# Node order worked out in eight pieces inside the loop over h, with ScalarE taking half of each node's row

## The chip, the cores and the metric

The kernel runs on one core of a Trainium2 chip. A core has five engines that run side by side and wait for one another through semaphores: TensorE (PE, with its weight loads shown apart as PEld), VectorE (DVE), ScalarE (ACT), GpSimd (POOL) and SyncE (SP). The last three can also issue DMAs. The metric is the device time of one execution in microseconds; lower is better.

## The reference, cut to what matters

Four layers of a graph network over 2048 nodes and 8 batches of 64 features. Only the start of the first layer matters here:

```python
h = x @ W                                     # (8, 2048, 64)
s = leaky_relu(h @ a_node, 0.2)
alpha = softmax(where(H.T > 0, s, NEG))       # weights of the nodes in each of 64 hyperedges
agg = einsum('ben,bnf->bef', alpha, h)        # what the edges gather from their nodes
beta = sigmoid((h @ a_gn)[:, None, :] + (agg @ a_ge)[:, :, None])
all_he = elu(beta * h + (1 - beta) * agg)     # one row for each pair of node and edge
```

A later stage (here the mixing stage) needs, for each node, a row with h scaled by `exp(h @ a_gn)`, and it needs the nodes sorted by how many edges they belong to, so that tiles of 128 nodes have equal numbers of edges.

## The kernel before, in words

**The loop over h (lines 597 to 645)** goes over 16 tiles of 128 nodes, `t` = 0 to 15. In each round:

- PE multiplies the tile of x by the weights: four matmuls into the PSUM tile `ph` (line 600). `ph` has two buffers; each fills two PSUM banks, k = 0 and k = 1, with four batches each.
- DVE clips the two score columns into `seen` (line 611); ACT takes the exponential of one of them into `e_gn`, which is part of the row tile `st` (line 616); DVE makes the leaky relu `lr` (618) and ACT its exponential into `ex` (622).
- DVE writes the node's row into `st`, (h + 1) · e_gn, with one instruction of 256 columns for each bank (625), and h times the softmax weight into `ex` (629).
- PE adds `ex` into the edges' sums `pagg` with two matmuls (637).
- POOL copies the slot numbers into `st` (614). `st` holds two tiles and has three buffers, so a buffer is free again when the store from three pairs ago has landed.
- In odd rounds ACT's queue issues the store of two tiles of rows, `hs_hbm` (635). After rounds 1, 3, 5, 7 and 9 POOL copies one element of `seen` (`behind`, line 482) and then issues a 512 KB load of the adjacency, `load_adj` (211): that copy is what paces the loads. After rounds 9 and 11 `parts` splits a block of x in two (ACT cast, line 167, and POOL subtraction, line 168).

**The nodes' order.** After round 9, `place()` (lines 553 to 590) works out the sorted position of each node: ten small DVE instructions, one large DVE comparison (`ohq`, 128x2048, line 578), 16 small matmuls into `po` (582) and two more DVE instructions, which write `order`.

**After the loop**, POOL gathers the sorted rows from `hs_hbm` with indirect DMAs (`fetch_rows`, line 275), which need `order` and all eight stores, and issues the remaining loads of the adjacency (tiles 10 to 15, columns half 0, then half 1 a few at a time). DVE, ACT and PE turn `pagg` into the edges' tables (lines 672 to 733): `den`, `agg`, `he`, `tab`, then scores `pse`, then `ts`. The first mixing step needs `ts` (line 717) and one-hot matrices `o` (line 294), which are made from the slot numbers of the first gathered row tile (`pslot`, `slot`, lines 285 to 288).

From there on PE interleaves the mixing steps with the products of the adjacency (`ug`, lines 383 to 418), a fixed number of them behind each step, and the later layers follow.

**What sets the order of the work.** Each engine runs its instructions in the order in which they stand on its queue. A scheduler decides that order when the program is built, except for instructions that are wrapped in `tc.keep_in_program_order`, which stay in the order of the program on their engine. In the loop of the kernel before, only ACT's exponential of `lr` is wrapped (line 621); `mm` (line 171) is a matmul that is wrapped.

Of the kernel before, what the change touches and what calls it, by code (L numbers as in the profile page):

```python
# [30 lines left out]
F32 = mybir.dt.float32  # L31
F32R = mybir.dt.float32r
BF16 = mybir.dt.bfloat16
# [3 lines left out]
AF = mybir.ActivationFunctionType  # L37
ALU = mybir.AluOpType
AX = mybir.AxisListType
# [17 lines left out]
def tile_gnn_fast(  # L57
# [24 lines left out]
    nc = tc.nc  # L82
    B, N, F = out.shape
    E = h_nt.shape[2]
    D = emb.shape[1]
    P = 128
    NT = N // P
# [116 lines left out]
    order = hy.tile([P, NT], U32, name="order")  # L204
# [130 lines left out]
    def fetch(p, c, eng=nc.sync):  # L335
        xc[p, c] = staged("xc")
        load_x(xc[p, c], p, c, eng)

    def parts(p, c):
        part[c] = split(va, xc.pop((p, c)), f"v{c}", 1, [P, JT, P], nc.gpsimd, p == 0)  # L340
# [94 lines left out]
    with tc.tile_pool(name="pa_ps", bufs=1, space=PSUM) as pps:  # L435
# [10 lines left out]
        m_n = pa.tile([P, NT, E], F32, name="m_n")  # L446
# [18 lines left out]
        so = so_scope.enter_context(tc.tile_pool(name="so", bufs=1))  # L465
# [4 lines left out]
        iota = so.tile([P, P], BF16, name="iota")  # L470
        nc.gpsimd.iota(iota, [[1, P]], base=0, channel_multiplier=0, allow_small_or_imprecise_dtypes=True)
        row = so.tile([P, 1], F32, name="row")
# [8 lines left out]
        def behind(what):  # L481
            tc.keep_in_program_order(nc.gpsimd.tensor_copy(seen_x, what))
# [6 lines left out]

        for c in range(2):  # L490
            fetch(0, c, nc.gpsimd)
        paced = {1: 5, 3: 6, 5: 7, 7: 8, 9: 9}

        pw = pps.tile([P, 2], F32, tag="sm", name="pw", bufs=2)
        nc.tensor.matmul(pw, lhsT=w0t, rhs=a2, start=True, stop=True)
        for b in range(2):
# [21 lines left out]
            flat, lhsT=tri, rhs=oh.rearrange("p t b -> p (t b)"), start=True, stop=False  # L518
        )
        for t in range(NT - 1):  # L520
            nc.tensor.matmul(
                flat[:, (t + 1) * BINS:], lhsT=ones_b,
                rhs=oh[:, t:t + 1, :].to_broadcast([P, NT - 1 - t, BINS]), start=False, stop=False,
            )
        nc.tensor.matmul(
            flat, lhsT=ones_b, rhs=gtb[:, None, :].to_broadcast(bins), start=False, stop=True
# [4 lines left out]
        rank = so.tile([P, NT], F32, name="rank")  # L531
        nc.vector.tensor_reduce(rank, gt, AX.X, ALU.add)

        over = so.tile([P, BINS], F32, name="over")
# [9 lines left out]
        for t in range(NT // 2):  # L544
            for k in range(2):
                r = slice(k * E, (k + 1) * E)
# [3 lines left out]
        slot = pa.tile([P, NT, E], BF16, name="slot")  # L550
        nc.vector.tensor_tensor(slot, pcm, m_n, ALU.mult)

        def place():

            tl = so.tile([P, NT], F32, name="tl")
            ge = so.tile([P, NT, NT], F32, name="ge")
            tc.keep_in_program_order(
                nc.vector.tensor_scalar(over[:, 0:NT], iota[:, 0:NT], float(P), -0.5, op0=ALU.mult, op1=ALU.add)
            )
            wide = [P, NT, NT]  # L560
            nc.vector.tensor_tensor(
                ge, rank[:, :, None].to_broadcast(wide), over[:, None, 0:NT].to_broadcast(wide), ALU.is_gt
            )
            nc.vector.tensor_reduce(tl, ge, AX.X, ALU.add)
            nc.vector.tensor_scalar(tl, tl, -1.0, None, op0=ALU.add)
            q = so.tile([P, NT], F32, name="q")
            nc.vector.scalar_tensor_tensor(q, tl, -float(P), rank, op0=ALU.mult, op1=ALU.add)
            nc.vector.tensor_tensor(
                ge, tl[:, :, None].to_broadcast(wide), iota[:, None, 0:NT].to_broadcast(wide), ALU.is_equal
            )  # L570
            val = so.tile([P, NT, 2, NT], BF16, name="val")
            nc.vector.tensor_tensor(
                val[:, :, 0, :], ge, iota[:, 0:NT, None].to_broadcast(wide), ALU.mult
            )
            nc.vector.tensor_scalar(val[:, :, 1, :], ge, row, None, op0=ALU.mult)
            po = pps.tile([P, 2, NT], F32, tag="sm", name="po", bufs=2)
            ohq = so.tile([P, NT, P], BF16, name="ohq")
            nc.vector.tensor_tensor(
                ohq, q[:, :, None].to_broadcast([P, NT, P]), iota[:, None, :].to_broadcast([P, NT, P]), ALU.is_equal
            )  # L580
            for t in range(NT):
                nc.tensor.matmul(
                    po.rearrange("p i t -> p (i t)"), lhsT=ohq[:, t, :],
                    rhs=val[:, t].rearrange("p i t -> p (i t)"), start=t == 0, stop=t == NT - 1,
                )
            olo = so.tile([P, NT], F32, name="olo")
            nc.vector.tensor_copy(olo, po[:, 1, :])

            nc.vector.scalar_tensor_tensor(order, olo, float(NT), po[:, 0, :], op0=ALU.mult, op1=ALU.add)
            so_scope.close()  # L590


        seen = pa.tile([P, NT, B, 2], F32, name="seen")

        pagg = pps.tile([P, C], F32, tag="agg", name="pagg", bufs=1)
        G = B // 2
        for t in range(NT):
            ph = pph.tile([P, 2, C], F32, tag="ph", name="ph", bufs=2)
            for p in range(NP):
                nc.tensor.matmul(  # L600
                    ph[:, p // 2, (p % 2) * 2 * (F + 2):(p % 2 + 1) * 2 * (F + 2)], lhsT=xt[t][:, p, :],
                    rhs=bd66.rearrange("p b f -> p (b f)"), start=True, stop=True,
                )
            fetch_xt(t + 2 * XB)
            hv = ph[:, :, 0:G * (F + 2)].rearrange("p k (g c) -> p k g c", c=F + 2)
            if t % 2 == 0:
                st2 = pa.tile([P, 2, HROW], F32, tag="st", name="st", bufs=3)
            st = st2[:, t % 2]
            ex = pa.tile([P, 2, G, F + 1], F32, tag="ex", name="ex", bufs=2)
            sv = seen[:, t].rearrange("p (k g) c -> p k g c", k=2)  # L610
            nc.vector.tensor_scalar(
                sv, hv[:, :, :, F:F + 2], CLIP, -CLIP, op0=ALU.min, op1=ALU.max
            )
            nc.gpsimd.tensor_copy(st[:, BF + 8:], slot[:, t, :])
            e_gn = st[:, BF:BF + 8]
            nc.scalar.activation(e_gn.rearrange("p (k g) -> p k g", k=2), sv[:, :, :, 1], AF.Exp)
            lr = pa.tile([P, B], F32, tag="lr", name="lr", bufs=2)
            nc.vector.scalar_tensor_tensor(
                lr, seen[:, t, :, 0], 0.2, seen[:, t, :, 0], op0=ALU.mult, op1=ALU.max
            )  # L620
            tc.keep_in_program_order(
                nc.scalar.activation(ex[:, :, :, F], lr.rearrange("p (k g) -> p k g", k=2), AF.Exp)
            )
            for k in range(2):
                nc.vector.scalar_tensor_tensor(
                    st[:, k * G * F:(k + 1) * G * F].rearrange("p (g f) -> p g f", f=F), hv[:, k, :, 0:F], 1.0,
                    e_gn[:, k * G:(k + 1) * G, None].to_broadcast([P, G, F]), op0=ALU.add, op1=ALU.mult,
                )
            nc.vector.tensor_tensor(
                ex[:, :, :, 0:F], hv[:, :, :, 0:F], ex[:, :, :, F:F + 1].to_broadcast([P, 2, G, F]), ALU.mult  # L630
            )
            if t == 9:
                place()
            if t % 2:
                nc.scalar.dma_start(hs_hbm.rearrange("(p t) c -> p t c", t=NT)[:, t - 1:t + 1, :], st2)
            for k in range(2):
                nc.tensor.matmul(
                    pagg[k * E:(k + 1) * E, 0:G * (F + 1)], lhsT=m_n[:, t, :], rhs=ex[:, k].rearrange("p g c -> p (g c)"),
                    start=t == 0, stop=t == NT - 1,
                )  # L640
            if t in paced:
                behind(seen[:, t, 0, 0:1])
                load_adj(paced[t], 0)
            if t in (9, 11):
                parts(0, (t - 9) // 2)
        nc.vector.tensor_reduce(
            wrong[:, 2:3], seen.rearrange("p t b c -> p (t b c)"), AX.X, ALU.max, apply_absolute_value=True
        )
# [93 lines left out]
    with ExitStack() as pb_scope:  # L742
        pps = pb_scope.enter_context(tc.tile_pool(name="pb_ps", bufs=1, space=PSUM))
# [311 lines left out]
    for i in range(steps + 1):  # L1055
        k = 9 if i > NCH else 8
# [536 lines left out]
    for u in range(2, UNITS):  # L1593
        c, k = divmod(u, 2)
# [134 lines left out]
    place = ["g"] * NCH  # L1729
# [63 lines left out]
    for p in range(NP):  # L1793
# [3 lines left out]
        for step in range(STEPS):  # L1797
            last = step == STEPS - 1
            w_v, bias = (bd_v, b1) if step == 0 else (bd_v2, b1s)
            if p == 0 and step == 0:  # L1800
                opened = opening()
            for g in range(2):
# [16 lines left out]
                for mine in ([[c] for c in own] if very_end else [own]):  # L1819
                    for t in range(NT if p or step else 0):  # L1820
                        if checks and t in (2, 7, 12):
                            check()
                        for i in range(2):
                            for c in mine:
                                mm(
                                    u[c], lhsT=x_part[t // JT][i][:, t % JT, :], rhs=adj_c(t, c),
                                    start=False, stop=t == NT - 1 and i == 1,
# [765 lines left out]
```

## Time and profile before

| what | us |
|---|---|
| median of 3 runs | 1750.76 (1748.91 to 1751.80) |
| the profiled execution's own time | 1754.68 |
| its span | 1752.8 |
| PE busy in the span | 1670.7 (95%) |
| DVE, ACT, POOL busy | 855.4, 600.9, 572.4 |
| first `seen` of the loop over h starts | 14.45 |
| last store of rows is issued | 55.63 |
| last `pagg` starts | 56.12 |
| first gather of sorted rows is issued | 59.28 |
| first one-hot matrix of the mixing stage starts | 65.27 |

Times of single events are counted from the start of the span. A row of the timeline gives start, duration (of the whole group where it ends in xN), engine, line, operation, output and inputs, shapes, and in brackets how long the engine had been idle and what ended that. In the table of stretches, each line gives the busy time of PE, PEld, DVE, ACT and POOL with the number of instructions, the clock that was granted to TensorE (1.00 is full), the share of the DMA engines' time and the rate of the DMAs.

### The profile page before, as it was taken

Reading aid. Unit: us, or ns where it says so; the run is one execution under the profiler, and the core shown is the slowest. Engines: PE = TensorE matmul, PEld = TensorE weight load, DVE = VectorE, ACT = ScalarE, POOL = GpSimd, SP = SyncE. Lnnn points to the kernel's source line nnn. Section 1 sums busy time; section 2 is a strip of 40 time slices with the busy share of each in tenths; the row PEclk is TensorE's granted clock in tenths of the full one; section 3 lists DMA queues with packets and bytes.
Section 4 is the critical chain, followed back from the end, with each engine's and each line's share of the span. In section 5 each row is a group of like instructions: output and inputs, shape, how many; then the busy total and the mean of one; then the engine's idle time right before and its main releaser. Section 6 shows DMA issues by size and latency. Waiting matters only on the chain. (4 is left out here: it accounts for less than half of the span.)

```text
span 1752.8 us, 28206 instructions
## 1 busy us (share of the span) xinstructions
PE 1670.7 (95%) x11196; PEld 1214.0 (69%) x11196; DVE 855.4 (49%) x1583; ACT 600.9 (34%) x1123; POOL 572.4 (33%) x515
## 2 busy tenths in 40 slices
PE   6888899999889999999999999999989999999996
PEld 4666666666664444468788877777767877878775
DVE  7679945678742221210137158888723433433332
ACT  1345524434221211111213158888612222222221
POOL 4578845556534443422023001222310200202001
PEclk9899999999989999999999989999999999999998
DMA  9743344444340000027344467576481121211211
GB/s 328 252 161 124 101 130 140 152 143 144 99 135 6 30 19 12 24 69 292 109 137 130 115 134 153 125 162 139 126 295 42 49 60 44 61 43 44 59 42 39
DMA packets 171182, 195.84 MB, mean 112 GB/s; under 512 B 71536, under 2 KB 116336, under 8 KB 169760
## 3 DMA queue, kind: packets, MB, share of 16 engines
q1 hardware_dynamic: 160096, 154.54, 30.3%
q0 software_dynamic: 8544, 30.68, 5.2%
q10 hardware_dynamic: 2400, 8.72, 1.4%
q8 instruction: 90, 1.47, 0.3%
q14 instruction: 52, 0.43, 0.1%
HBM read 126.72 MB, written 67.17 MB: 111 GB/s over the span
## 5 line engine op out<-in xcount | busy, mean ns | idle before, releaser
L172 PE MATMUL ua<-pt,xn 128*128 128x512 f32 x512 | 230.2, 592 | 1.4 <-DVE pt L1150 1.4
L1488 ACT COPY w_half<-pw 128x512 f32<-128x512 f32 x316 | 191.3, 687 | 44.9 <-PE pw L172 43.4
L172 PEld LDWEIGHTS ua<-pt,xn 128*128 128x128 f32 x512 | 96.9, 190 | 111.1 <-issue 104.0
L1490 DVE COPY w_half<-pw 128x512 f32<-128x512 f32 x196 | 133.7, 715 | 72.7 <-PE pw L172 70.2
L172 PE MATMUL py<-w_half,xg 128*32 128x128 f32 x4096 | 142.6, 281 | 0.0
L172 PE MATMUL u<-adj,v0h 128*128 128x512 f32 x384 | 134.0, 426 | 1.1 <-ACT h L1788 1.1
L172 PE MATMUL u<-adj_more,v2h 128*128 128x512 f32 x384 | 126.5, 408 | 0.0
L172 PE MATMUL u<-adj_more,v2l 128*128 128x512 f32 x384 | 125.0, 403 | 0.0
L172 PE MATMUL u<-adj,v0l 128*128 128x512 f32 x384 | 124.5, 402 | 0.0
L172 PEld LDWEIGHTS py<-w_half,xg 128*32 128x32 f32 x4096 | 111.8, 138 | 17.4 <-issue 0.4
L172 PE MATMUL pw<-est,wst 64*128 64x256 f32 x1024 | 118.3, 324 | 4.1 <-DMA est<-est_hbm 2.3
L1156 POOL TENSOR_TENSOR acc<-acc,pt 128x512 f32<-128x512 f32 x60 | 76.5, 1276 | 104.2 <-DVE pt L1150 103.5
L172 PEld LDWEIGHTS pw<-est,wst 64*128 64x128 f32 x1024 | 82.8, 189 | 35.6 <-issue 18.5
L1150 DVE TENSOR_SCALAR pt<-pt 128x512 f32<-128x512 f32 x64 | 29.7, 465 | 152.6 <-ACT pt L1149 152.4
L1697 ACT CAST ar<-fcav 128x512 fp32r<-128x512 f32 x64 | 39.5, 618 | 166.7 <-DMA fcav<-in_adj_t 162.0
L1698 DVE SCALAR_TENSOR_TENSOR ar<-fcav,ar 128x512 f32<-128x512 f32 x64 | 45.6, 713 | 101.2 <-ACT ar L1697 101.0
L172 PE MATMUL u<-adj,v1h 128*128 128x512 f32 x288 | 94.6, 407 | 0.0
L1149 ACT ACTIVATE pt<-s 128x512 f32<-128x512 f32 x64 | 38.0, 598 | 164.5 <-PE s L172 164.5
L172 PE MATMUL u<-adj_more,v3l 128*128 128x512 f32 x288 | 93.9, 401 | 0.0
L172 PE MATMUL u<-adj_more,v3h 128*128 128x512 f32 x288 | 93.2, 402 | 0.0
L172 PE MATMUL u<-adj,v1l 128*128 128x512 f32 x288 | 92.7, 400 | 0.0
L1669 POOL TENSOR_TENSOR x<-x,rows 128x512 f32<-128x512 f32 x16 | 22.5, 1432 | 210.6 <-PE pt L175 200.2
(405 smaller groups left out, 3220.0 us busy)
## 6 DMA issues: line engine op xcount, KB each, us to landing
fcav<-in_adj_t SPq DMA_DIRECT2D x64, 256.0 KB, 2.9
u_hbm<-ut SPq DMA_DIRECT2D x48, 256.0 KB, 2.6
xg<-u_hbm SPq DMA_DIRECT2D x24, 512.0 KB, 9.0
adj<-in_adj_t POOLq DMA_DIRECT2D x16, 512.0 KB, 7.6
adj_more<-in_adj_t POOLq DMA_DIRECT2D x16, 512.0 KB, 7.5
adj_hbm<-adj_more SPq DMA_DIRECT2D x16, 512.0 KB, 6.1
x_hbm<-r SPq DMA_DIRECT2D x28, 256.0 KB, 2.8
hs_hbm<-st ACTq DMA_DIRECT2D x8, 584.0 KB
```

The source lines that it names most:

```text
L172: tc.keep_in_program_order(nc.tensor.matmul(*args, **kw))
L1149: nc.scalar.activation(pt, s, AF.Exp)
L1150: nc.vector.tensor_scalar(pt, pt, 1.0, None, op0=ALU.max)
L1156: nc.gpsimd.tensor_tensor(accs[c], accs[c], pt, ALU.add)
L1488: pin(nc.scalar.copy(dst, src))
L1490: pin(nc.vector.tensor_copy(dst, src))
L1669: nc.gpsimd.tensor_tensor(xs, xs, b2.to_broadcast([P, JT, P]), ALU.add)
L1697: nc.scalar.copy(ar, seen_a)
L1698: nc.vector.scalar_tensor_tensor(ar.bitcast(F32), seen_a, 1.0, ar.bitcast(F32), op0=ALU.mult, op1=ALU.not_equal, accum_out=left[:, t, k:k ...
```

## The change

Four things are done in the loop over h.

- `place()` is cut into eight pieces that are put at the ends of rounds 4 to 11: `find_tile` (4), `tile_columns` (5), four pieces of `row_columns` with a quarter of `ohq` each (6 to 9), `turn_order` with the 16 matmuls (10), `write_order` (11).
- The half of a node's row in bank k = 1 is written by ACT, with one instruction of 64 columns for each of four batches: `Identity(scale · h + bias)` with scale and bias both the column `e_gn` of that batch. DVE keeps the half in bank k = 0.
- The loop's instructions on PE, DVE and ACT are wrapped so that they stay in the program's order, and the program issues `pagg` of round t - 1 in round t (`gather`).
- Four more loads of the adjacency are paced in the loop, tiles 10 to 13, behind `seen` of rounds 11, 12, 13 and 14.

In the order of the built program, PE's instructions stand as before, except that the 16 `po` matmuls come one round earlier. DVE goes round by round: `seen`, `lr`, `st`, `ex`, then the round's piece. ACT goes `e_gn`, `ex`, four Identities, and in odd rounds the store's issue. The first of the four Identities waits for DVE's half of the same row. On POOL the copies of slots for rounds 6 and 7 now stand ahead of the pacing copy of round 3, and the four loads stand ahead of the first gather.

```diff
-        paced = {1: 5, 3: 6, 5: 7, 7: 8, 9: 9}
+        paced = {1: 5, 3: 6, 5: 7, 7: 8, 9: 9, 11: 10, 12: 11, 13: 12, 14: 13}
...
-        def place():
...
+        hold = tc.keep_in_program_order
+        def find_tile():
+            hold(nc.vector.tensor_scalar(over[:, 0:NT], iota[:, 0:NT], float(P), -0.5, op0=ALU.mult, op1=ALU.add))
+            hold(nc.vector.tensor_tensor(ge, rank..., over..., ALU.is_gt))
+            hold(nc.vector.tensor_reduce(tl, ge, AX.X, ALU.add))
+            hold(nc.vector.tensor_scalar(tl, tl, -1.0, None, op0=ALU.add))
+            hold(nc.vector.scalar_tensor_tensor(q, tl, -float(P), rank, op0=ALU.mult, op1=ALU.add))
+        def tile_columns():       # ge, then two halves of val
...
+        def row_columns(i):
+            r, quarter = slice(i * NT // 4, (i + 1) * NT // 4), [P, NT // 4, P]
+            hold(nc.vector.tensor_tensor(ohq[:, r, :], q[:, r, None]..., iota..., ALU.is_equal))
+        def turn_order():         # 16 matmuls into po
...
+        def write_order():        # olo, order
...
+        placing = {4: find_tile, 5: tile_columns, 10: turn_order, 11: write_order}
+        for i in range(4):
+            placing[6 + i] = lambda i=i: row_columns(i)
...
-            for k in range(2):
-                nc.vector.scalar_tensor_tensor(st[...], hv[:, k, :, 0:F], 1.0, e_gn[...], op0=ALU.add, op1=ALU.mult)
-            nc.vector.tensor_tensor(ex[:, :, :, 0:F], hv[:, :, :, 0:F], ex[:, :, :, F:F + 1]..., ALU.mult)
-            if t == 9:
-                place()
+            hold(nc.vector.scalar_tensor_tensor(st[:, 0:G * F]..., hv[:, 0, :, 0:F], 1.0, e_gn[:, 0:G, None]..., op0=ALU.add, op1=ALU.mult))
+            for g in range(G, B):
+                one = e_gn[:, g:g + 1]
+                hold(nc.scalar.activation(st[:, g * F:(g + 1) * F], hv[:, 1, g - G, 0:F], AF.Identity, bias=one, scale=one))
+            hold(nc.vector.tensor_tensor(ex[:, :, :, 0:F], hv[:, :, :, 0:F], ex[:, :, :, F:F + 1]..., ALU.mult))
+            if t in placing:
+                placing.pop(t)()
+            if t > 0:
+                gather(t - 1)
```

More of the change, by code (lines that the diff above doesn't have):

```diff
@@ L551, in tile_gnn_fast @@
         nc.vector.tensor_tensor(slot, pcm, m_n, ALU.mult)
-        def place():
[L555 to L580, printed above, removed]
@@ new lines, in tile_gnn_fast @@
+        wide_t = [P, NT, NT]
+        tl, q, olo = (so.tile([P, NT], F32, name=name) for name in ("tl", "q", "olo"))
+        ge = so.tile(wide_t, F32, name="ge")
+        val = so.tile([P, NT, 2, NT], BF16, name="val")
+        ohq = so.tile([P, NT, P], BF16, name="ohq")
+        po = pps.tile([P, 2, NT], F32, tag="sm", name="po", bufs=2)
+        hold = tc.keep_in_program_order
+        def find_tile():
+            hold(nc.vector.tensor_scalar(over[:, 0:NT], iota[:, 0:NT], float(P), -0.5, op0=ALU.mult, op1=ALU.add))
+            hold(nc.vector.tensor_tensor(
+                ge, rank[:, :, None].to_broadcast(wide_t), over[:, None, 0:NT].to_broadcast(wide_t), ALU.is_gt
+            ))
+            hold(nc.vector.tensor_reduce(tl, ge, AX.X, ALU.add))
+            hold(nc.vector.tensor_scalar(tl, tl, -1.0, None, op0=ALU.add))
+            hold(nc.vector.scalar_tensor_tensor(q, tl, -float(P), rank, op0=ALU.mult, op1=ALU.add))
@@ new lines, in tile_columns @@
+        def tile_columns():
+            hold(nc.vector.tensor_tensor(
+                ge, tl[:, :, None].to_broadcast(wide_t), iota[:, None, 0:NT].to_broadcast(wide_t), ALU.is_equal
+            ))
+            hold(nc.vector.tensor_tensor(
+                val[:, :, 0, :], ge, iota[:, 0:NT, None].to_broadcast(wide_t), ALU.mult
+            ))
+            hold(nc.vector.tensor_scalar(val[:, :, 1, :], ge, row, None, op0=ALU.mult))
+        def row_columns(i):
+            r, quarter = slice(i * NT // 4, (i + 1) * NT // 4), [P, NT // 4, P]
+            hold(nc.vector.tensor_tensor(
+                ohq[:, r, :], q[:, r, None].to_broadcast(quarter), iota[:, None, :].to_broadcast(quarter),
+                ALU.is_equal,
+            ))
@@ L581, in place @@
+        def turn_order():
             for t in range(NT):
-                nc.tensor.matmul(
+                mm(
                     po.rearrange("p i t -> p (i t)"), lhsT=ohq[:, t, :],
@@ L585, in place @@
                 )
-            olo = so.tile([P, NT], F32, name="olo")
-            nc.vector.tensor_copy(olo, po[:, 1, :])
-            nc.vector.scalar_tensor_tensor(order, olo, float(NT), po[:, 0, :], op0=ALU.mult, op1=ALU.add)
+        def write_order():
+            hold(nc.vector.tensor_copy(olo, po[:, 1, :]))
+            hold(nc.vector.scalar_tensor_tensor(order, olo, float(NT), po[:, 0, :], op0=ALU.mult, op1=ALU.add))
             so_scope.close()
+        placing = {4: find_tile, 5: tile_columns, 10: turn_order, 11: write_order}
+        for i in range(4):
+            placing[6 + i] = lambda i=i: row_columns(i)
         seen = pa.tile([P, NT, B, 2], F32, name="seen")
@@ L596, in tile_gnn_fast, with gather @@
         G = B // 2
+        exs = {}
+        def gather(t):
+            ex = exs.pop(t)
+            for k in range(2):
+                mm(
+                    pagg[k * E:(k + 1) * E, 0:G * (F + 1)], lhsT=m_n[:, t, :], rhs=ex[:, k].rearrange("p g c -> p (g c)"),
+                    start=t == 0, stop=t == NT - 1,
+                )
         for t in range(NT):
@@ L599, in tile_gnn_fast @@
             for p in range(NP):
-                nc.tensor.matmul(
+                mm(
                     ph[:, p // 2, (p % 2) * 2 * (F + 2):(p % 2 + 1) * 2 * (F + 2)], lhsT=xt[t][:, p, :],
@@ L610, in tile_gnn_fast @@
             sv = seen[:, t].rearrange("p (k g) c -> p k g c", k=2)
-            nc.vector.tensor_scalar(
+            hold(nc.vector.tensor_scalar(
                 sv, hv[:, :, :, F:F + 2], CLIP, -CLIP, op0=ALU.min, op1=ALU.max
-            )
+            ))
             nc.gpsimd.tensor_copy(st[:, BF + 8:], slot[:, t, :])
             e_gn = st[:, BF:BF + 8]
-            nc.scalar.activation(e_gn.rearrange("p (k g) -> p k g", k=2), sv[:, :, :, 1], AF.Exp)
+            hold(nc.scalar.activation(e_gn.rearrange("p (k g) -> p k g", k=2), sv[:, :, :, 1], AF.Exp))
             lr = pa.tile([P, B], F32, tag="lr", name="lr", bufs=2)
-            nc.vector.scalar_tensor_tensor(
+            hold(nc.vector.scalar_tensor_tensor(
                 lr, seen[:, t, :, 0], 0.2, seen[:, t, :, 0], op0=ALU.mult, op1=ALU.max
-            )
+            ))
             tc.keep_in_program_order(
@@ L623, in tile_gnn_fast @@
             )
-            for k in range(2):
[L625 to L629, printed above, removed]
-                ex[:, :, :, 0:F], hv[:, :, :, 0:F], ex[:, :, :, F:F + 1].to_broadcast([P, 2, G, F]), ALU.mult
-            )
-            if t == 9:
-                place()
+            hold(nc.vector.scalar_tensor_tensor(
+                st[:, 0:G * F].rearrange("p (g f) -> p g f", f=F), hv[:, 0, :, 0:F], 1.0,
+                e_gn[:, 0:G, None].to_broadcast([P, G, F]), op0=ALU.add, op1=ALU.mult,
+            ))
+            for g in range(G, B):
+                one = e_gn[:, g:g + 1]
+                hold(nc.scalar.activation(
+                    st[:, g * F:(g + 1) * F], hv[:, 1, g - G, 0:F], AF.Identity, bias=one, scale=one
+                ))
+            hold(nc.vector.tensor_tensor(
+                ex[:, :, :, 0:F], hv[:, :, :, 0:F], ex[:, :, :, F:F + 1].to_broadcast([P, 2, G, F]), ALU.mult
+            ))
+            if t in placing:
+                placing.pop(t)()
+            if t > 0:
+                gather(t - 1)
+            exs[t] = ex
             if t % 2:
                 nc.scalar.dma_start(hs_hbm.rearrange("(p t) c -> p t c", t=NT)[:, t - 1:t + 1, :], st2)
[L636 to L640, printed above, removed]
             if t in paced:
@@ L645, in tile_gnn_fast @@
                 parts(0, (t - 9) // 2)
+        gather(NT - 1)
         nc.vector.tensor_reduce(
```

## The prediction

> **What bounds the kernel now.** I read the busy table first (PE 95% of the span), so work that is taken from other engines counts only where PE stands still for them. The table of stretches shows where that is: the start.
>
> ```profile
> 12.00:26.00 14.00, 12.06 (x78) 9.28 (x72) 10.11 (x31) 2.11 (x10) 3.67 (x12) 0.88 1.08 376
> 26.00:36.00 10.00, 8.81 (x62) 5.88 (x61) 8.33 (x27) 2.04 (x11) 2.58 (x10) 1.00 1.00 364
> 36.00:42.50 6.50, 2.66 (x32) 1.91 (x32) 6.34 (x19) 1.04 (x4) 4.86 (x7) 1.00 0.74 238
> 42.50:56.80 14.30, 11.07 (x57) 6.88 (x53) 8.61 (x25) 3.44 (x13) 1.44 (x3) 0.76 0.42 157
> 67.00:77.00 10.00, 9.46 (x29) 7.77 (x30) 6.83 (x14) 3.81 (x14) 6.91 (x9) 0.51 1.08 375
> ```
>
> PE is busy 2.66 of 6.5 us while DVE works out the nodes' order; the DMAs are full until 36 us (share 1.00 and above) and half empty after 42.5, and PE's granted clock there is 0.76. ACT is nearly idle. Then I read the timeline: a steady round, the order, and the end.
>
> ```profile
> 24.33 0.17 DVE L611 TENSOR_SCALAR seen<-ph 128x16 f32<-128x16 f32 x1
> ...
> 24.53 0.21 ACT L616 ACTIVATE st<-seen 128x8 f32<-128x8 f32 x1 [1.21 <-DVE seen L611]
> ...
> 24.77 0.76 DVE L625 SCALAR_TENSOR_TENSOR st<-ph,st 128x256 f32<-128x256 f32 x2
> ...
> 25.06 1.17 PE L600 MATMUL ph<-firsts,xt 128*128 128x132 f32 x8
> 25.44 0.68 DVE L629 TENSOR_TENSOR ex<-ph,ex 128x512 f32<-128x512 f32 x1
> ...
> 26.26 0.17 DVE L611 TENSOR_SCALAR seen<-ph 128x16 f32<-128x16 f32 x1
> ...
> 37.82 2.32 DVE L578 TENSOR_TENSOR ohq<-q,iota 128x2048 bf16<-128x2048 f32 x1
> ...
> 42.19 0.17 DVE L611 TENSOR_SCALAR seen<-ph 128x16 f32<-128x16 f32 x1
> ...
> 55.63 0.33 ACTq L635 DMA_DIRECT2D hs_hbm<-st  x1
> ...
> 56.12 0.66 PE L637 MATMUL pagg<-ex,m_n 128*64 128x260 f32 x4 [1.47 <-DVE ex L629]
> ...
> 59.28 1.13 POOL L275 DMA_INDIRECT hrow<-hs_hbm,order  x1 [13.39 <-DVE he L680]
> ...
> 65.07 0.16 DVE L717 TENSOR_TENSOR ts<-tsm,tsr 64x8 fp32r<-64x8 f32 x1
> 65.27 1.81 DVE L294 TENSOR_SCALAR o<-slot 128x128 fp32r<-128x128 bf16 x12
> ```
>
> `seen` starts at 14.45 for the first time, then at 24.33, 26.26, 27.98, 29.91 and 31.68: 1.84 us a round, DVE and PE both nearly full. From 14.45 to the last `pagg` (56.12) are 41.7 us: 15 rounds at 1.84 (27.6), 2.0 behind the last `seen`, and 12 us of stalls. The stalls, by the starts of `seen`: 2.5 in the first four rounds, 4.2 at the order (36.19 to 42.19 is one round), 4.5 in rounds 11 to 15 (42.19 to 54.10), where the scheduler put `seen` of round 13 ahead of `st` of round 12 and PE's eight `ph` matmuls take 2.13 us twice instead of 1.17; the rest is a wait for a store (2.06 us on ACT at 32.68). After the loop two chains run to the first one-hot `o` at 65.27: edges' tables up to `ts` (from 56.12, ends 65.23) and stores, gather, slots (from 55.63; the gathered rows land at 62.83, their transposition `pslot` stands behind `pse` on PE and starts at 63.53). The tables end last, the rows have 0.7 us to spare. From `o` on PE has work waiting, and the rest of the program shifts as a whole.
>
> **The change, part by part.** Durations are those of the profiled execution.
>
> DVE in a steady round: `seen` to `st` 0.44, one half of `st` instead of two (0.41 alone at 55.05; the next starts 0.33 later), `ex` 0.62 to the next start: 1.39 against 1.73 before. So a piece of up to 0.5 us hides.
>
> ACT in a steady round is the new cost. The trace has no Identity with two column operands; the nearest groups are these.
>
> ```profile
> L299 ACT ACTIVATE far<-slot,number 128x128 bf16<-128x128 bf16 x45 | 15.8, 392 | 0.4
> L300 ACT ACTIVATE o<-far 128x128 fp32r<-128x128 bf16 x45 | 11.6, 296 | 0.1
> ```
>
> Same shape, one with a bias column: a column costs 96 ns. PSUM as source saves 31 (copies of 512 columns: 587 against casts from SBUF at 618), 64 columns fewer save 53 (0.84 ns each, between PSUM copies of 512 at 587 and of 256 at 373). Without columns 296 - 31 - 53 = 212; with one 308, with two 404 ns. The bounds are 212 and 404; I take 404, as two columns are read. Two `y` in a row take 1.08 us at 0.60 each, so starts overlap by 0.10: four Identities take 3 x 0.31 + 0.40 = 1.33. In the Trainium skill ("ScalarE: Activation LUTs", What ACT_TABLE_LOAD costs) each column operand adds about 93 ns to 186 + 0.833 N, which would make 425 ns, 1.42 us for four and 1.4 us more over the loop than I take. The same page (Rules for kernel authors) says that add and mul belong on VectorE, not ScalarE, which speaks against this edit; here DVE's half costs 0.41.
>
> The first Identity waits for DVE's half: `seen` + 0.44 + 0.41 + 0.05 = + 0.90; the four end at + 2.23, and ACT can start the next `e_gn` at + 2.14, that is 1.94 after this one's (+ 0.20). In odd rounds the store is issued behind them (0.05 + 0.33 + 0.04): 2.45. Queued behind the Identities on ACT are the next `e_gn`, for which DVE's `st` waits, and the store. So a pair of rounds takes 4.39, a round 2.2: the steady round gets *slower* by 0.35, bound by ACT; PE (1.13 + 0.59 = 1.72) and DVE wait for it.
>
> What goes: the stalls. The order on DVE costs 1.34 in round 4 (0.17 + 0.41 + 0.42 + 0.17 + 0.17), 1.21 in round 5, 0.58 (2.32/4) in rounds 6 to 9, 0.34 in round 11. Only rounds 4 and 5 pass ACT's 2.2: 2.73 and 2.60, so 0.5 + 0.4. The `po` matmuls take 0.55 on PE, hidden. If ACT were faster, all 5.2 would show against 1.72. The kept order costs nothing and ends the mix-up of rounds 12 and 13. Stores: a buffer returns after three pairs, 13.2 us, and a landing takes 6.5 to 8.6 us under load (20.41 to 26.9, 23.98 to 32.6); with 4.4 for filling it that is 13.0 at most, so the wait of 32.68 goes too.
>
> The sum: 7 pairs and one round 32.7, rounds 4 and 5 0.9, two casts of `parts` on ACT 1.2, half-clock PE in rounds 2 and 3 (18.14 to 20.76 is 2.6 a round against 2.2) 0.8, from the last `seen` to `pagg` 1.7 (its `wrong` reduction adds 0.2): 37.3, so `pagg` starts at 51.8 instead of 56.1, 4.3 earlier. The last store is issued at 14.45 + 35.6 + 2.5 = 52.5, 3.1 earlier. With landing and gather as before (3.6 and 3.6) the rows land at 59.7; `pslot` 0.3 and two `slot` copies 0.65 end at 60.7, `ts` at 60.9. Both chains meet: about 4.3 earlier.
>
> The four loads (0.5 MB each) move ahead on POOL's queue, past the first gather and the split of blocks 2 and 3. Their issue (0.55) and pacing copies (0.2) lie in a POOL that is busy 1.44 of 14.3 us. At 0.4 MB/us they and the stores of rounds 11 and 13 need 8 us of DMA from about 43 on, just done at 52. What they cost the last store and the gather is between nothing (3.6 as now) and 5 (8.6, a landing under load); since they end about when the store starts I take 0.3. The third gather, which now lands 10.4 us after its issue behind six loads, comes earlier, but its rows are used only at 89.5: nothing. The POOL copies for rounds 6 and 7 ahead of the pacing copy of round 3 delay one load by 1 to 2 us; it is used after 57: nothing.
>
> Later stages change by a few reordered DVE and ACT instructions in the mixing stage: 1 us to either side, I take 0. The gain is 4.0 us: 1754.7 becomes 1750.7. This execution was 3.9 over the median of 1750.8, so the forecast is **1746.8**, 0.23% less. A measurement can tell about 0.2% (3.5 us) from no change, so this lies at the edge.
>
> **The rivals.**
>
> *ScalarE is cheaper, or PE keeps its clock.* With one column's cost (308, starts 0.21 apart) Identities take 0.94, a pair 3.6, and PE's 1.72 is near: `pagg` would come about 6 earlier, the store 5. And the half clock from 67 to 77, in which PE is busy 9.46 of 10 us, could fall away when PE arrives with fewer pauses: up to 4 us. For: the two columns are one; against: the 96 ns, and the small matmuls before 67 stay as they are. 1741 to 1744.
>
> *The tail gives it back.* The last store and first gather meet the moved loads. At a landing of 6.5 to 8.6 instead of 3.6 the rows land 3 to 5 later, and the gain is 0 to 1: 1750. For: one queue serves loads and gathers in order; against: the DMA share of 0.42 there.
>
> *Slower: ACT's Identities.* Each 10 ns on an Identity costs 0.6 us in 64 of them. The gain is gone at about 470 ns. If ACT and DVE, which now read the same PSUM bank at once (`ex` and the Identities), hold each other up, to 550 ns say, the loop ends 9 us later than forecast: 5 slower, 1756. For: before, ACT read nothing of `ph`; against: no row shows such a slowdown.
>
> That ACT takes the work but the steady pace stays, so that nothing moves, is within the first two.
>
> **How the numbers follow.** Forecast (gain 2 to 6.5): 0.55, of which 0.40 is above 3.5 us. Cheaper ACT or kept clock: 0.19, all faster. Tail: 0.13, within 0.2%. Slower: 0.13, of which 0.02 within. Faster 0.59, same 0.30, slower 0.11. The range goes from 1741.5, into the first rival, to 1752.0, past the tail's no gain and as far as Identities of 490 ns; it leaves out some 0.05 below and 0.10 above. The forecast's own range is 1744.3 to 1748.8.
>
> **What would show it.** Right: `seen` every 2.2 us in rounds 9 to 15 with ACT as releaser, Identities of 0.40, no gap of DVE at the order, last `pagg` near 51.8, last store near 52.5, first gather near 56, `o` near 61. Wrong: Identities above 0.47; the last store landing more than 5 us after its issue; `o` at 61 but the span not 4 shorter, which would mean that the mixing stage waits for something else, a load or the clock.

## The result: slower, because `ex` waits for the Identities

The changed kernel takes 1760.74 us (median of 6 runs, 1758.89 to 1764.94), the kernel before 1752.09 beside it (6 runs, 1748.91 to 1755.90): ratio 1.0057, interval 1.0044 to 1.0071. The forecast was 1746.8, the range ended at 1752.0. The two profiled executions differ by less, 1758.89 against 1754.68: that of before is slower than five of these six, that of after is the fastest of its six.

Of each view only the lines that the argument needs are shown. The timeline of the changed kernel, one steady round (round 3, 23.6 to 26.5 us), the piece and the end of round 4, and the end:

```profile
23.60 0.16 DVE L631 TENSOR_SCALAR seen<-ph 128x16 f32<-128x16 f32 x1
24.04 0.42 DVE L644 SCALAR_TENSOR_TENSOR st<-ph,st 128x256 f32<-128x256 f32 x1
24.56 1.29 ACT L650 ACTIVATE st<-ph,st 128x64 f32<-128x64 f32 x4 [0.29 <-DVE st L644]
25.88 0.69 DVE L653 TENSOR_TENSOR ex<-ph,ex 128x512 f32<-128x512 f32 x1 [1.42 <-ACT st L650]
26.49 0.16 DVE L631 TENSOR_SCALAR seen<-ph 128x16 f32<-128x16 f32 x1
26.63 0.66 PE L172 MATMUL pagg<-ex,m_n 128*64 128x260 f32 x4 [1.14 <-DVE ex L653]
...
29.38 0.16 DVE L562 TENSOR_SCALAR over<-iota 128x16 f32<-128x16 bf16 x1
...
30.79 0.17 DVE L631 TENSOR_SCALAR seen<-ph 128x16 f32<-128x16 f32 x1
...
67.23 0.33 ACTq L662 DMA_DIRECT2D hs_hbm<-st  x1
67.93 0.66 PE L172 MATMUL pagg<-ex,m_n 128*64 128x260 f32 x4 [2.39 <-DVE ex L653]
71.39 1.16 POOL L275 DMA_INDIRECT hrow<-hs_hbm,order  x1 [8.31 <-DMA hs_hbm<-st]
75.78 0.28 PE L175 MATMUL pslot<-ident,hrow 128*64 128x128 f32 x1
77.21 0.16 DVE L740 TENSOR_TENSOR ts<-tsm,tsr 64x8 fp32r<-64x8 f32 x1
77.41 1.80 DVE L294 TENSOR_SCALAR o<-slot 128x128 fp32r<-128x128 bf16 x12
```

Read the brackets of one round downwards: the Identities had waited for DVE's half of `st`, and `ex` had waited for the Identities. `seen`, `st`, four Identities and `ex` stand in one line, 2.89 us from `seen` to `seen` (23.60 to 26.49), and DVE idles 1.42 us in the middle. Since `ex` ends the round on DVE, the order's piece comes behind it and adds its whole length: 1.41 us in round 4 (29.38 to 30.79). The last `pagg` starts at 67.93 instead of 56.12.

The table of waits of the changed kernel, 14 to 68 us (who waited for whom: us in total, times, longest):

```profile
PEld pagg L172 <- DVE ex L653: 24.6, 15, 2.9
DVE ex L653 <- ACT st L650: 23.0, 16, 1.8
PE pagg L172 <- DVE ex L653: 21.2, 14, 2.5
ACT st L650 <- DVE st L644: 4.8, 14, 0.7
```

All 16 rounds wait, 23.0 us together. PE waits in turn, and the table of stretches shows it: PE is busy 3.63 of 5.75 us in two steady rounds (6.98 of 7.35 in four steady rounds before, 24.33 to 31.68).

```profile
20.74:26.49 5.75, 3.63 (x24) 2.29 (x24) 2.70 (x9) 3.43 (x12) 0.54 (x3) 0.96 0.87 319
52.80:67.93 15.13, 7.69 (x53) 4.89 (x53) 7.37 (x24) 9.52 (x32) 4.21 (x9) 1.00 0.73 234
68.90:72.30 3.40, 3.40 (x11) 2.48 (x10) 3.02 (x10) 1.56 (x5) 0.91 (x1) 0.51 0.18 74
```

Of the 12.1 us by which `o` comes later (77.41 against 65.27), 7.5 are left at the last multiplication of the PSUM tile `pz` on DVE, near the end of the mixing stage (233.1 against 225.6). The third line bears on that: between 60 and 90 us before had a granted clock of 0.50 (the half clock, from here on) for 10.2 us, from 66.5 on, after for 3.4 us twice (from 68.9 and from 79.2). The 3.4 us less are an estimated 1.7 us of work at half speed. What gave back the rest was not settled.

### The profile page after: what moved, and what is told of

The parts are those of the page before. It is cut to its first block, busy times and chain, and to the rows that moved or that the text cites. A ratio compares the mean times of both kernels' runs of the same rounds, so it can differ in the third digit from the quotient of the medians.

```text
span 1757.1 us, 28278 instructions
## 1 busy us (share of the span) xinstructions
PE 1664.6 (95%) x11196; PEld 1208.8 (69%) x11196; DVE 849.9 (48%) x1570; ACT 621.5 (35%) x1187; POOL 571.8 (33%) x519
```

## The experiments

Theory: the loss is `ex`'s wait for the Identities, and the other three parts of the change are gains or nothing. Rivals: the pieces or the kept order cost time; the moved loads do; or ACT and DVE slow each other when both read `ph`.

**DVE writes both halves**, all else as changed:

```diff
-            hold(nc.vector.scalar_tensor_tensor(st[:, 0:G * F]..., hv[:, 0, :, 0:F], ...))
-            for g in range(G, B): ... AF.Identity ...
+            for k in range(2):
+                hold(nc.vector.scalar_tensor_tensor(st[:, k * G * F:...], hv[:, k, :, 0:F], ...))
```

> The changed kernel with one edit undone: DVE writes both halves of the row, ScalarE none. Theory (the four Identities stand on DVE's own path, because ex waits for the last of them): without them a round falls from 2.9 us to about 1.75 to 1.85, the pieces of the order add their 5 us once, the last pagg starts near 51.5 instead of 67.9, and the whole is 3 to 6 us faster than the kernel before. Rival A (the eight pieces, the kept orders or the regrouped pagg cost the time): the loop stays near 60 us or later and the whole stays 5 us or more slower than before. Rival B (the four loads ahead of the gather give it back): the loop is short but the gathered rows land late, and the whole is within 2 us of before.

1746.61 us, ratio to before 0.9971 (0.9960 to 0.9982). Timeline of this kernel:

```profile
20.27 0.16 DVE L631 TENSOR_SCALAR seen<-ph 128x16 f32<-128x16 f32 x1
20.71 0.76 DVE L645 SCALAR_TENSOR_TENSOR st<-ph,st 128x256 f32<-128x256 f32 x2
21.39 0.68 DVE L649 TENSOR_TENSOR ex<-ph,ex 128x512 f32<-128x512 f32 x1
22.20 0.17 DVE L631 TENSOR_SCALAR seen<-ph 128x16 f32<-128x16 f32 x1
```

Two DVE instructions in 0.76 us replace 0.42 + 1.29 + gaps; no bracket is left in the round. A round takes 1.93 here (1.7 to 2.0 in the first four, which have no piece), the last `pagg` comes at 50.40, 17.5 us earlier than in the changed kernel, and no half clock falls into the loop. So the other three parts together are a gain, and the Identities alone turn the change into a loss.

**ScalarE's half alone**, put into the kernel before:

```diff
-            for k in range(2):
-                nc.vector.scalar_tensor_tensor(st[...], hv[:, k, :, 0:F], ...)
+            nc.vector.scalar_tensor_tensor(st[:, 0:G * F]..., hv[:, 0, :, 0:F], ...)
+            for g in range(G, B):
+                nc.scalar.activation(st[:, g * F:(g + 1) * F], hv[:, 1, g - G, 0:F], AF.Identity, bias=one, scale=one)
```

> The kernel before with ScalarE's half alone: no pieces, no kept orders, no loads. Theory (the Identities stand on DVE's path): slower than before even alone, though the scheduler puts seen of the next round ahead of ex and so hides a part of the wait: a round of 2.3 to 2.7 us instead of 1.84, the last pagg 4 to 12 us later than 56.1, the whole 2 to 9 us slower. Rival A (the pieces or the kept orders cost, and ScalarE's half is harmless): the same time as before, within 2 us.

1767.83 us, ratio 1.0087 (1.0069 to 1.0106); last `pagg` at 74.75, later by 18.6. Both are outside the expected spans: 17 us slower where 2 to 9 were expected, and 18.6 where 4 to 12 were. The timeline of this kernel shows why it is worse than the whole change:

```profile
16.89 2.48 ACT L630 ACTIVATE st<-ph,st 128x64 f32<-128x64 f32 x8 [0.18 <-DVE st L624]
18.22 0.69 DVE L633 TENSOR_TENSOR ex<-ph,ex 128x512 f32<-128x512 f32 x1 [1.10 <-ACT st L630]
20.03 2.13 PE L600 MATMUL ph<-firsts,xt 128*128 128x132 f32 x8
22.20 0.17 DVE L611 TENSOR_SCALAR seen<-ph 128x16 f32<-128x16 f32 x1 [2.10 <-PE ph L600]
```

Without the kept order the scheduler takes two rounds at once, both `ph` buffers are held until ACT's eight Identities are through, PE stops and its eight matmuls then take 2.13 us at the half clock (1.17 at full clock); the granted clock over the loop is 0.76. With the kept order and the pieces, but without the moved loads (last experiment), the last `pagg` comes at 67.36; which of the two limits the damage is not shown.

**`ex` issued ahead of the Identities:**

```diff
+            hold(nc.vector.tensor_tensor(ex[:, :, :, 0:F], hv[:, :, :, 0:F], ...))
             for g in range(G, B): ... AF.Identity ...
-            hold(nc.vector.tensor_tensor(ex[:, :, :, 0:F], hv[:, :, :, 0:F], ...))
```

> The changed kernel with ex issued ahead of the four Identities; work and instruction counts are the same. Theory: DVE no longer waits for ScalarE in a round; the Identities wait for ex instead, ACT's chain e_gn, DVE's st, ex, four Identities takes about 2.5 us, and the last pagg starts near 59.5, 8 us earlier than in the changed kernel; the whole is 0 to 4 us slower than the kernel before. Rival A: the order of these two does not matter, the last pagg stays near 68. Rival C (ScalarE and DVE slow each other on the same PSUM tile): Identities or ex get longer than 1.29 us for four and 0.69.

1754.61 us, ratio 1.0018 (1.0007 to 1.0030); last `pagg` at 60.15. DVE no longer waits in the middle of a round, but ACT's next exponential stands behind the Identities, and PE's next matmuls wait for the buffer that they still read. Waits of this kernel, 14 to 62 us:

```profile
DVE st L644 <- ACT st L636: 18.3, 14, 2.0
PE ph L172 <- ACT st L653: 9.1, 12, 1.1
```

**Two batches instead of four by ScalarE:**

```diff
+            hold(nc.vector.scalar_tensor_tensor(st[:, G * F:(B - 2) * F]..., hv[:, 1, 0:G - 2, 0:F], ...))
-            for g in range(G, B):
+            for g in range(B - 2, B):
```

> The changed kernel with ScalarE writing two of the eight batches of a row instead of four; DVE writes six, with one more instruction of 128 columns. Theory: ex waits for two Identities instead of four, a round is about 0.4 us shorter than 2.9 (0.6 less on ACT, 0.2 more on DVE), the last pagg starts near 61.5, and the whole lies 3 to 7 us above the kernel before, about half way between the changed kernel and the one without Identities. Rival A: no change against the changed kernel.

1754.39 us, ratio 1.0012 (0.9998 to 1.0026); a round takes 2.5 and the last `pagg` comes at 61.72. Its timeline:

```profile
23.56 0.70 ACT L654 ACTIVATE st<-ph,st 128x64 f32<-128x64 f32 x2 [0.50 <-DVE st L648]
24.29 0.69 DVE L657 TENSOR_TENSOR ex<-ph,ex 128x512 f32<-128x512 f32 x1 [0.85 <-ACT st L654]
```

Two Identities take 0.70 instead of 1.29, and `ex` waits 0.85 for them instead of 1.42. So the last `pagg` comes the later, the more Identities there are: none 50.4, two 61.7, four 67.9.

**`ex` cut by bank**, in two instructions, bank 0 first:

```diff
-            hold(nc.vector.tensor_tensor(ex[:, :, :, 0:F], hv[:, :, :, 0:F], ...))
+            for k in range(2):
+                hold(nc.vector.tensor_tensor(ex[:, k, :, 0:F], hv[:, k, :, 0:F], ...))
```

> The changed kernel with DVE's ex cut in two instructions, bank k = 0 and then bank k = 1. The question is what ex waits for. Theory A (the order is kept for ph as one tensor of two banks, whatever bank an instruction reads): the half of bank 0 also waits for the fourth Identity, although the Identities read only bank 1; the round stays at 2.9 us and grows by the second instruction, the last pagg comes at 68 to 70 (67.9 in the changed kernel). Rival (the order is kept bank by bank): the half of bank 0 runs beside the Identities, only the half of bank 1 waits, a round takes 2.6 and the last pagg comes at about 63.

One run, 1767.52, so without an interval; last `pagg` at 68.41. Its timeline:

```profile
24.43 1.30 ACT L650 ACTIVATE st<-ph,st 128x64 f32<-128x64 f32 x4 [0.28 <-DVE st L644]
25.76 0.76 DVE L654 TENSOR_TENSOR ex<-ph,ex 128x256 f32<-128x256 f32 x2 [1.42 <-ACT st L650]
```

The first half reads only bank 0 and the Identities only bank 1, yet it waits the same 1.42. In this program the order is kept for `ph` as a whole.

**A tensor for each bank**, so that only readers of the same bank are ordered:

```diff
-            ph = pph.tile([P, 2, C], F32, tag="ph", name="ph", bufs=2)
+            ph = (pph.tile([P, 2, C], F32, tag="ph", name="ph", bufs=2)[:, 0],
+                  pps.tile([P, C], F32, tag="ph1", name="ph1", bufs=2))
...
+            weigh(1)          # ex, bank 1; then the four Identities, then st and ex of bank 0
...
+            weigh(0)
```

> The changed kernel with the two banks of ph as two tensors (two buffers each; the small PSUM tiles of this stage get one buffer instead of two, which makes the chain behind the loop 1 to 3 us longer), seen in two instructions and ex in two: DVE goes ex of bank 1, st of bank 0, ex of bank 0, and ACT's Identities start behind ex of bank 1. Nothing of DVE waits for an Identity of the same round. Theory (what the change lost is the wait, not a slowdown of engines that read different banks side by side): four Identities stay at 1.3 us and DVE's instructions at their lengths while they overlap; ACT then bounds the round as forecast, seen to seen 2.3 to 2.5; last pagg at 55 to 59, against 67.9 in the changed kernel and 50.4 where DVE writes both halves; so even without the wait the edit is no gain. Rival (engines that read PSUM side by side hold each other up): Identities of more than 1.5 for four or DVE instructions 20 per cent longer, last pagg above 62. The time should then be 5 to 9 us below that of the changed kernel (about 1752 to 1756).

1756.35 us, ratio 1.0024 (1.0009 to 1.0039). Timeline:

```profile
27.75 0.42 DVE L647 TENSOR_TENSOR ex<-ph,ex 128x256 f32<-128x256 f32 x1 [0.34 <-ACT ex L644]
28.09 0.41 DVE L656 SCALAR_TENSOR_TENSOR st<-ph,st 128x256 f32<-128x256 f32 x1
28.27 1.29 ACT L653 ACTIVATE st<-ph,st 128x64 f32<-128x64 f32 x4 [0.55 <-DVE ex L647]
28.42 0.42 DVE L647 TENSOR_TENSOR ex<-ph,ex 128x256 f32<-128x256 f32 x1
...
55.59 0.66 PE L172 MATMUL pagg<-ex,m_n 128*64 128x260 f32 x4 [1.39 <-DVE ex L647]
```

DVE reads bank 0 while ACT reads bank 1, and neither is longer for it: 1.29 for four Identities, 0.41 and 0.42 on DVE. In program order DVE's `st` and `ex` of bank 0 stand behind the Identities, and they no longer wait for them. Now ACT bounds the round (`ex` waits 11.0 us in 16 rounds for ACT's exponential, which stands behind the Identities of the round before), two rounds without a piece take 4.7 us (16.19 to 20.85, within the 2.3 to 2.5 a round expected), and the last `pagg` comes at 55.59. That is within the 55 to 59 expected, 12.3 us earlier than with the wait and 5.2 later than with DVE alone: even a split without the wait is no gain at the end of the loop. (The time is 0.4 above the expected span. The chain behind the loop is longer, 11.2 us from `pagg` to `o` against 9.5: 0.9 up to the scores `pse`, with one buffer for the small PSUM tiles, and 0.8 behind them, where DVE's small `wrong` takes 1.42 us instead of 0.17 beside a subtraction on POOL.)

**The order whole after round 9**, in the kernel of the first experiment:

```diff
-        placing = {4: find_tile, 5: tile_columns, 10: turn_order, 11: write_order}
-        for i in range(4): ...
+        placing = {9: place}       # all eight pieces one after the other
```

> As the run without Identities, and the order is worked out in one go after round 9 again, its instructions kept in the program's order. It tells what the eight pieces are worth alone. Theory: DVE is nearly full in both, so the pieces move 5.2 us of DVE work about without hiding it; what they save is PE's standstill of 4 us and the half clock behind it: the last pagg starts 1 to 3 us later than with the pieces. Rival A (the pieces are what costs): it is as fast as or faster than the run with the pieces.

1750.15 us, ratio 0.9993 (0.9984 to 1.0002); last `pagg` at 52.63, 2.2 later than in pieces. Against 56.12 before, the kept order (with the moved loads) is worth 3.5 at the last `pagg`, though the one round that holds the whole order is longer than before (10.2 us from `seen` to `seen`, 30.93 to 41.15, against 6.0). The time shows nothing of the 3.5, its interval takes in 1: the last store lands 7.6 us after its issue, `pslot` waits 4.0 for the gathered rows, and `o` starts at 66.00 against 65.27 before. In the medians the pieces are worth 3.5 (1746.61 against 1750.15).

**The moved loads**, twice: the kernel of the first experiment without the four, and with them early.

```diff
-        paced = {1: 5, 3: 6, 5: 7, 7: 8, 9: 9, 11: 10, 12: 11, 13: 12, 14: 13}
+        paced = {1: 5, 3: 6, 5: 7, 7: 8, 9: 9}                           # without
+        paced = {1: 5, 3: 6, 5: 7, 7: 8, 8: 9, 9: 10, 10: 11}            # early, two of the four
```

> The run without Identities, and without the four extra loads in the loop (tiles 10 to 13 are loaded after the first two gathers, as before). In the run with them the last store took 7.2 us from 49.9 to land, against 3.6 before, and PE waited 3.3 us for the gathered rows. Theory (the tail gives part of the gain back): here the last store lands within 4 us, the first gather is issued near 54, the first one-hot near 60 instead of 63.1, and the whole is 2 to 4 us faster than with the loads. Rival (the late landing has another cause, or the loads cost as much behind the gather): same first one-hot, or an equal whole.

> The run without Identities, with two of the four extra loads, and these earlier: tiles 9, 10 and 11 behind rounds 8, 9 and 10, none behind rounds 11 to 14. Theory: the last store meets fewer loads and lands in about 4 us, so the first one-hot comes near 60 as in the run without extra loads; the stores of rounds 7 to 11 may land later and make a round wait by 1 to 2 us. Rival: the loads cost the same wherever they are, and the first one-hot stays near 63.

1744.99 us, ratio 0.9959 (0.9944 to 0.9974), and 1744.67 us, ratio 0.9968 (0.9953 to 0.9982). The intervals overlap with that of the first experiment (0.9960 to 0.9982), so in time the three are not told apart, and the 2 to 4 us expected of leaving the loads out are not shown; in the traces they are told apart. The waits behind the loop in the first experiment's kernel:

```profile
POOL hrow L275 <- DMA hs_hbm<-st: 10.1, 1, 10.1
PEld pslot L175 <- DMA hrow<-hs_hbm,order: 3.3, 1, 3.3
```

The stretch ahead of the last store, in that kernel and then in the one without the loads (DMA share is the last but one number):

```profile
42.50:49.80 7.30, 5.17 (x36) 3.33 (x36) 6.99 (x19) 1.34 (x7) 4.00 (x10) 1.00 0.97 272
```

```profile
42.50:49.80 7.30, 5.50 (x40) 3.63 (x40) 6.51 (x20) 1.89 (x10) 1.27 (x1) 1.00 0.63 229
```

The first gather without the loads, from the timeline:

```profile
52.79 1.18 POOL L275 DMA_INDIRECT hrow<-hs_hbm,order  x1 [8.94 <-DVE he L699]
```

With the loads the DMA share is 0.97 when the last store is issued (49.86); it lands 7.2 us later, the gather starts at 57.9, `pslot` makes PE wait 3.3 and `o` starts at 63.07. Without them the store lands 2.8 us after its issue, the gather starts at 52.79 and `o` at 58.83; with two loads early it lands after 3.9, the gather starts at 54.65 and `o` at 59.97, though the last `pagg` (50.39) is no earlier than with the four. So the chain behind the loop is 3 to 4 us shorter, and what becomes of that later is open.

**The changed kernel without the four loads:**

```diff
-        paced = {1: 5, 3: 6, 5: 7, 7: 8, 9: 9, 11: 10, 12: 11, 13: 12, 14: 13}
+        paced = {1: 5, 3: 6, 5: 7, 7: 8, 9: 9}
```

> The changed kernel without the four extra paced loads. In the changed kernel the last store landed 3.3 us after its issue, as in the kernel before, so the loads had drained in the long loop. Theory: no difference, within 2 us of the changed kernel (1758.5 to 1762.5). Rival (the moved loads are part of the loss, through the DMA share in the loop or the gathers): 3 us or more below it.

1764.23 us, ratio 1.0069 (1.0050 to 1.0089), against 1.0057 (1.0044 to 1.0071) with them: no gain, as expected, though the median is 1.7 us above the span given. So no part of the loss is seen to come from the loads: in the long loop of the changed kernel they have drained, and the last store lands 3.3 us after its issue.

## Why the prediction was wrong

**The step that failed** is a wait that the forecast put at nothing: "DVE in a steady round: ... 1.39" has `ex` straight behind `st`, with no wait for the Identities, so DVE's 1.39 lay beside ACT's 1.94 and only the next `e_gn` and the store had to come after the Identities. In the program that was built, `ex` waits for the fourth Identity, 1.42 us in a steady round and 23.0 us in all. The `ex` cut by bank and the kernel with a tensor for each bank show the reason: both read `ph`, and although neither writes there, readers on two engines are put in an order. The chain is `seen` 0.44, `st` 0.42, Identities 1.29, `ex` 0.61, with the hand-overs 2.89. The order of instructions on each engine, which the section on the change tells, doesn't show this: it holds the queues. Of the waits between them that section names the one of the first Identity for DVE's half, and the forecast priced it; the one back, of `ex` for the last Identity, it does not name.

The Trainium skill has the rule that I should have weighed: by "PSUM — Partial Sum Buffer" (PSUM bank collisions raise a hardware error), two engines may not touch the same bank in the same 32 partitions at once, reads against reads included, so such pairs have to be ordered. That bears on `ex` and the Identities in bank 1, and the 23.0 us of waits fit it; the page's other half, that different banks don't disturb each other, agrees with the unchanged 1.29 and 0.42 in the kernel with a tensor for each bank. The wait of bank 0's half (1.42) is more than the page asks for. What a collision does, no run here shows.

Point by point:

| step | predicted | measured |
|---|---|---|
| one Identity; four of them | 0.404; 1.33 | 0.403; 1.29 |
| steady round | 2.2 | 2.89 |
| pieces of rounds 4 and 5 beyond a round | 0.5 + 0.4 | 1.41 + 1.05 |
| last `seen` to last `pagg` | 1.7 | 3.2 |
| last `pagg` | 51.8 | 67.9 |
| last store: issue; landing | 52.5; 3.9 later | 67.2; 3.3 later |
| `o` | 61 | 77.4 |

- The Identity was sized rightly, at the end of the bounds that two columns gave. The 425 ns by the Trainium skill's "ScalarE: Activation LUTs" (What ACT_TABLE_LOAD costs) are 5% above the 403 measured; with them the forecast would have kept the same wrong step.
- The 16.1 us between 51.8 and 67.9 come for the most part out of that one step: 15 rounds at 0.69 more (10.4); pieces that were to hide and don't, with what is left of casts and clock, 4.2 (50.2 us from the first `seen` to the last, less 35.6 forecast and 10.4); and 1.5 from the last `seen` to `pagg`. Of the 4.2, 0.7 is another thing, a round 10 in which `lr` took 1.03 us beside POOL's subtraction (last section).
- Not all of it was the wait. In the kernel with a tensor for each bank, where `ex` waits for no Identity, the last `pagg` still comes 3.8 us later than forecast (55.59 against 51.8). A pair of rounds takes 4.7 there (4.39 forecast), and rounds 4 to 11 with the pieces take 22.9 (22.89 to 45.77), where the forecast for them adds up to 19.7 (four pairs at 4.39, 0.9 and 1.2). So in that kernel the pieces don't hide behind ACT as forecast; its DVE has two instructions more in a round, and what these do to the pieces was not measured.
- "Slower: ACT's Identities" pointed at the right place, `ex` and the Identities on the same bank, but priced it as a slowdown of each instruction. They don't slow each other (1.29 for four Identities with and without a DVE instruction beside them), `ex` waits: 1.42 us a round instead of the 0.6 that the 9 us of this rival make.
- The rule that the prediction cites, that add and mul belong on VectorE (same page, Rules for kernel authors), holds here: DVE's second half costs 0.34 us more in a round (0.76 against 0.42) and replaces 1.29 on ACT with two hand-overs.
- "The kept order ... ends the mix-up" agrees with the kernel that has the order whole: from `seen` of round 11 to that of round 15 are 7.7 us (42.93 to 50.61) against 11.9 before (42.19 to 54.10), 4.2 less where 4.5 were put down to the mix-up. But the two groups of `ph` matmuls of 2.13 us, which the prediction counted to the mix-up, ran at the half clock (before had it from about 42.6 and from 49.4, for 3.4 us each), and the other kernel had none there, so order and clock are not told apart. On the pieces, "If ACT were faster, all 5.2 would show" was right: with DVE writing both halves rounds 4 to 11 take 19.7 us (22.20 to 41.88), 5.1 more than eight like its first four (1.82). Cutting the order still gains 2.2 over leaving it whole.
- "The tail gives it back" didn't decide here, but is real: with the fast loop the store landed 7.2 us after its issue, inside the 6.5 to 8.6 that I gave to this rival. My 0.3 for the loads was met by luck: the store met drained queues behind a loop that was 16 us longer than forecast, and behind the loop of the first experiment, 1.4 us shorter than forecast, the loads cost it 4.4 us (7.2 against 2.8 without them).
- "Later stages ... 0": the changed kernel caught up 4.6 of 12.1 us by 233 us. The clock accounts for an estimated 1.7 of it; half-clock windows came at other times in nearly every kernel.

**The better version** is the change without ScalarE's half: 0.3% faster than the kernel before with the four loads, 0.3 to 0.4% without them or with two of them early (1744.99 and 1744.67 us against 1750.48), and about 0.9% faster than the changed kernel. That fewer loads in the loop are better still, the times do not show.

## What to carry to other kernels

Before work is given to an idle engine, write down for each operand who else touches it, readers too: in this program two engines that only read the same PSUM tile took turns, whichever bank they read, and the help then stood in the helped engine's path (1.42 us a round against 0.34 saved). Read a built program for its waits, not only for its order on each engine. And cost a loop and its tail together: here the faster loop arrived at DMAs that had not drained (the last store landed 3.3 us after its issue behind the slow loop, 7.2 behind the fast one with the same loads).

## What the runs showed of the hardware that I had not expected

A DVE instruction of 0.17 us took 1.03 while POOL subtracted one 512-column tile from another. The timeline of the changed kernel:

```profile
49.09 1.31 POOL L168 TENSOR_TENSOR v0l<-xc,v0h 128x512 fp32r<-128x512 f32 x1 [2.12 <-ACT v0h L167]
49.39 1.03 DVE L638 SCALAR_TENSOR_TENSOR lr<-seen 128x8 f32<-128x8 f32 x1
```

It ends 0.02 after POOL's. In the kernel before, POOL's two slot copies took 2.61 us instead of 0.41 beside the large comparison on DVE (2.32 us from 37.82):

```profile
37.63 2.61 POOL L614 CAST st<-slot 128x64 f32<-128x64 bf16 x2 [1.68 <-DVE q L567]
```

The Trainium skill's "SBUF — State Buffer" (Who interferes with whom) says that a DVE instruction with two SBUF inputs and a GpSimd instruction that reads SBUF block each other, the later one for the whole of the earlier; both cases fit that.

The half clock came in windows of 3.4 us or near multiples of it. Up to the last `pagg` the changed kernel had 3.4 and 6.8 us of it, and ScalarE's half alone 27 us up to 71 us (3.4, 6.8 and 17.1). The loop of the first experiment had none, with PE busy 26.46 of 35.50 us. How much PE is busy in a loop does not settle it: the kernel before had 10.2 us of half clock with PE busy 31.47 of 41.67 us, and the kernel with a tensor for each bank none, with 27.18 of 41.63. What sets it off, no run here shows.
